# A two-layer graph network on one core: which engine copies the products out of PSUM, and how many tiles that engine fetches row by row

## The chip, the cores and the metric

The kernel runs on one core of a Trainium2 chip. The core has five engines with queues of their own: TensorE (PE), VectorE (DVE), ScalarE (ACT), GpSimd (POOL) and SyncE (SP, which here only issues transfers). Each engine works through its instructions in the order in which they were written. What is measured is the device time of one execution in microseconds (us), as the median of several runs. A comparison of this kernel can tell a difference of about 0.5% from none.

## The reference, cut to what matters

```python
# x: 50000 nodes x 128 floats; 850000 edges sorted by dst (400000 in both directions and 50000 self loops)
def layer(h, src, dst, rel, basis, w_comp, loop_w, bias):       # 16 relations, 8 bases
    W   = einsum('rb,bio->rio', w_comp, basis)
    agg = segment_sum(h[src], dst * 16 + rel)                   # sums of gathered rows by node and relation
    msg = einsum('nri,rio->no', agg.reshape(50000, 16, 128), W)
    return relu(msg + h @ loop_w + bias)
h = layer(x, ...1...); h = layer(h, ...2...)
out = layernorm(x + h)
```

What costs time is `h[src]`: in each layer one row of 512 bytes has to be fetched for each of the 800000 edges that are not self loops (self loops need no gather, since their row is the node's own).

## The kernel before, in words

The 800000 edges of a layer, sorted by destination, are cut into 6250 *tiles* of 128 edges. Five tiles are a *half chunk* (1250 a layer), two half chunks a *chunk* (625 a layer). `chunked()` runs over the two layers and, in each, over the chunks `c`. An order written out by hand (`tc.manual_schedule`) fixes the order on all five engines. The code that emits one tile also emits small steps of other work beside it (`beside`).

For each tile the 128 gathered rows come into a buffer `g` of 128 partitions. PE multiplies it with a matrix `hot` (L1145), which puts each edge's row into one of 12 local node columns for each of the 8 bases, weighted by the edge's relation. The five products of a half chunk fill one PSUM buffer `pa`; there are three such buffers. `taken_out()` (L1098 to L1101) copies a full `pa` to `aT` in SBUF. The call stands one tile late: it is emitted behind the first product of the next half chunk (L1154). In the first 8 and the last 8 chunks of a layer ScalarE makes this copy, in all others VectorE (`COPIED`, L1100).

Further work goes on beside: every fourth chunk PE multiplies `aT` with the bases (L816), ScalarE copies the result (`by_slot`, L821), PE transposes it (L826), VectorE spreads it (L799), and PE adds it into the nodes' sums (L861). For each group of 512 nodes the self loops are added (`hT` at L752, L766, L773, L781), and the group ends with a ReLU or a layer norm and a store (L883 to L896). VectorE makes the weights `hot` (L639, L668, L952).

Rows reach `g` on three ways. GpSimd fetches most tiles by one indirect gather of 128 rows each (L187). It fills a ring of 30 buffers (`RING * PER`); a slot is filled again when PE has used it, so the gathers run up to six half chunks ahead of PE. The row numbers for twenty tiles come from a ScalarE copy `at` (L1075). The last tile of some half chunks, though, is fetched row by row, as 128 transfers of 512 bytes, by SyncE or by ScalarE (`row_by_row`, L1048). Before every 32 rows the engine loads 32 addresses into registers (L1041) from the table `far` (L494). `takers()` deals these tiles out: SyncE takes the last tile of every ninth half chunk and so does ScalarE (`SPANS = (9, 9)`). That makes 136 tiles for SyncE and 135 for ScalarE in a layer. Their row transfers are spread evenly over the stretch of program that lies at least `LEAD = 8` half chunks ahead of the use. Each of the two engines has three buffers for such tiles. PE waits for the semaphore of a tile right at its product (L1145).

The tables of edges are made on the chip in groups (`rows_of`, L457). Group 0 holds the first 16 half chunks, group 1 the next 104. A generator `coming` makes the later groups a step at a time, and a loop at the head of a chunk (L1113) forces it to the end of a group when the group will soon be needed.

Of the kernel before, what the change touches and what calls it, by code (L numbers as in the profile page):

```python
# [60 lines left out]
LK = 64  # L61
LBITS = 10
FETCH = 2
WIDE = 20
AT = 8
PER = 5
Q = AT // 2
# [1 line left out]
WEIGHTS = AT * PER * 8  # L69
BITS_AT_ONCE = BANK - WEIGHTS  # L70
RING = 6
SPANS = (9, 9)
LEAD = 8
THEN = 3
COPIED = 8
HELD = 3
SEMS = 8
LOADED = 32
# [15 lines left out]
def tile_rgcn_resnorm(  # L94
# [15 lines left out]
    nc = tc.nc  # L110
# [4 lines left out]
    C = -(-M // (K * P))  # L115
# [4 lines left out]
    ROWS = list(range(0, 2 * C, P)) if 2 * C <= P else [0, FIRST, *range(P - 8, 2 * C, P)]  # L120
# [93 lines left out]
    uses = [0] * len(APART)  # L214
    earliest = (max(SPANS) + LEAD + 1) // 2 + 1
    far = consts.tile([P, len(ROWS), P], I32, name="far")

    def takers():

        of, first = {}, max(SPANS) + LEAD + 6  # L220
        for i, span in enumerate(SPANS):
            for q in range(first + span * i // len(SPANS), 2 * C - LEAD, span):
                while q in of:
# [388 lines left out]
    def chunked():  # L612
        with (
# [5 lines left out]
            def ks(c):  # L619
                return min(K, -(-M // P) - c * K)  # L620
# [26 lines left out]
            def told_apart(of, by, width, c, name):  # L647

                k = sum(ks(i) for i in range(c, min(c + Q, C)))
                apart = hp.tile([P, Q * K, width], U8, name=name, bufs=1)[:, :k]  # L650
                nc.vector.tensor_tensor(
                    apart,
                    of[:, None, :width].to_broadcast([P, k, width]),
                    by[:, c * K : c * K + k, None].to_broadcast([P, k, width]),
                    op=OP.is_equal,
                )
                return apart
# [241 lines left out]
            def done(steps):  # L899
                for _ in steps:  # L900
                    pass
# [19 lines left out]
            ready, read_by, numbered_all = [0], {}, []  # L921
# [18 lines left out]
            for n, of in enumerate((x, H1)):  # L940
# [78 lines left out]
                def alone(t):  # L1019

                    return t % PER == PER - 1 and t // PER in taken_by

                def row_by_row(i):
# [3 lines left out]
                    mine = sorted(q for q in taken_by if taken_by[q] == i)  # L1027
                    for q, before in zip(mine, [mine[0] - SPANS[i], *mine]):
                        while now[1] < before - LEAD:
# [25 lines left out]
                        held[q * PER + PER - 1] = to, sem, 16 * P * (use // SEMS + 1), group  # L1055
                        assert now[1] < q

                def place_in_ring(t):

                    turn, k = divmod(n * tiles + t, RING * PER)  # L1060
                    return k if turn % 2 == 0 else k // PER * PER + PER - 1 - k % PER
# [7 lines left out]
                def numbers(b):  # L1069

                    m = min(WIDE, tiles - b * WIDE)
                    if m <= 0:
                        return
                    at = hp.tile([P, WIDE], I32, name="at", bufs=3)[:, :m]
                    made = nc.scalar.copy(at, src[:, b * WIDE : b * WIDE + m])  # L1075
                    for group in read_by.pop(len(numbered_all) - 3, ()):
                        tc.declare_no_dep(made.ins, group=group, reason="their rows were used before")
                    read_by[len(numbered_all)] = read_now = []
                    numbered_all.append(at)
                    numbered[b] = at, read_now  # L1080

                def fetch(some):

                    for t in some:
                        if t < tiles:
                            if t % WIDE == WIDE // 2:
                                numbers(t // WIDE + 1)
                            if not alone(t):
                                at, read_now = numbered[t // WIDE]
                                k, group = place_in_ring(t), f"tile{n}_{t}"  # L1090
# [5 lines left out]
                to_take = []  # L1096

                def taken_out():  # L1098

                    by_vector = COPIED <= now[0] < C - COPIED  # L1100
                    (nc.vector.tensor_copy if by_vector else nc.scalar.copy)(*to_take)  # L1101

                numbered, held = {}, {}
                numbers(0)
                now, made = [0, 0], [0]
                owning = own_of_all()
                copying = [row_by_row(i) for i in range(len(APART))]
                for c in range(C):
                    now[0] = c
                    if n == 0 and c:  # L1110

                        next(coming, None)
                        while ready[0] + 1 < len(ROWS) and 2 * min(C, c + FETCH + earliest) > ROWS[ready[0] + 1]:  # L1113
                            next(coming)
                    if c == 0:
                        fetch(range(RING * PER))
                        nc.vector.tensor_copy(table, COMP[n].rearrange("p r b -> p b r"))
                        weighing = weights(0)
                        done(weighing)
                        hots[0] = hot_of(0)  # L1120
                        hots[1] = hot_of(1)
                        if n == 0:
                            for _ in range(LBITS + 3):
                                next(first_runs)
                    if c % 2 == 0 and c + 2 < C:
                        weighing = weights(c + 2)
                    hot = hots.pop(c)
                    if c % BATCH == 0:
                        aTs[c // BATCH] = hp.tile([P, NB, BATCH * S], F32, name="aT")
                    aT, place_of = aTs[c // BATCH], c % BATCH * S  # L1130
                    if c > ALONE:
                        done(summing)
                        summing = sum_up(c - 1)
                    elif c % BATCH == 0:
                        summing = slots_of_batch(c - BATCH, aTs[c // BATCH - 1], st, n) if c else iter(())
                    for k in range(0, K, PER):
                        m = min(PER, ks(c) - k)
                        if m > 0:
                            pa = ps_a.tile([P, BANK], F32, name="pa")
                        for i in range(PER):  # L1140
                            now[1] = 2 * c + k // PER
                            if i < m:
                                t = c * K + k + i
                                row, sem, count, group = held.pop(t)
                                product = nc.tensor.matmul(  # L1145
                                    pa[:, i * NB * WN : (i + 1) * NB * WN],
                                    row,
                                    hot[:, k + i].rearrange("e b w -> e (b w)"),
                                    start=True,
                                    stop=True,  # L1150
                                ).wait_op(sem, count, "sem-ge")
                                tc.declare_fence(product.ins, group=group)
                                tc.declare_no_dep(product.ins, group=group, reason="it waits for their semaphore itself")
                            if i == 0 and c + k:  # L1154
                                taken_out()
                            if i == m - 1:
                                at = c * K + k + RING * PER
                                fetch(range(at, at + PER))
                                if n == 0 and c == 0 and k == 0:
                                    done(first_runs)  # L1160
                                to_take[:] = [
                                    aT[:, :, place_of + k * WN : place_of + (k + m) * WN].rearrange(
                                        "d b (i w) -> d i b w", w=WN
                                    ),
                                    pa[:, : m * NB * WN].rearrange("d (i b w) -> d i b w", i=m, w=WN),
                                ]
                                if c * K + k + m == tiles:
                                    taken_out()
                            beside(k + i, c, owning, summing, weighing)
                    if c + 2 < C:  # L1170
                        hots[c + 2] = hot_of(c + 2)
                    for one in added_in(c + 1) if c + 1 < C else ():
                        masks[one] = masks_of(one)
                    if n == 0 and c == 3:
                        beginning.close()
                    if n == 0 and c == C - 1:
                        done(coming)
                        count_up(pr)
# [199 lines left out]
```

## Time and profile before

| | |
|---|---|
| median of 3 runs | 23771.16 us (23735.37 to 23829.01) |
| the profiled execution | 23546.47 us, its span 23544.3 us |
| PE busy | 11586.5 us (49%) |
| VectorE busy | 11688.0 us (50%) |
| GpSimd busy | 11364.1 us (48%) |
| ScalarE busy | 838.5 us (4%) |

No engine is counted as busy for more than half of the span. The page does not count instructions that issue transfers, though, and SyncE and ScalarE issue 17408 and 17280 row transfers in each layer. Whether they are full is read from the timeline, where such rows stand as SPq and ACTq with the number of transfers and the time from the first to the end of the last.

### The profile page before, as it was taken

Reading aid. Unit: us, or ns where it says so; the run is one execution under the profiler, and the core shown is the slowest. Engines: PE = TensorE matmul, PEld = TensorE weight load, DVE = VectorE, ACT = ScalarE, POOL = GpSimd, SP = SyncE. Lnnn points to the kernel's source line nnn. Section 1 sums busy time; section 2 is a strip of 40 time slices with the busy share of each in tenths; the row PEclk is TensorE's granted clock in tenths of the full one; section 3 lists DMA queues with packets and bytes.
Section 4 is the critical chain, followed back from the end, with each engine's and each line's share of the span. In section 5 each row is a group of like instructions: output and inputs, shape, how many; then the busy total and the mean of one; then the engine's idle time right before and its main releaser. Section 6 shows DMA issues by size and latency. Waiting matters only on the chain. (4 is left out here: it accounts for less than half of the span.)

```text
span 23544.3 us, 262043 instructions
## 1 busy us (share of the span) xinstructions
PE 11586.5 (49%) x43954; PEld 7419.2 (32%) x43954; DVE 11688.0 (50%) x14173; ACT 838.5 (4%) x1873; POOL 11364.1 (48%) x11991
## 2 busy tenths in 40 slices
PE   4544445444554544444554444444544444444445
PEld 3333333333333333233333333332332333333233
DVE  5555555555544444444544444444444444444445
ACT  0000000000000000000000000000000000000000
POOL 5544445444544444444454444444444444444444
PEclk7776677776677676676767776776766777766767
DMA  2111111111111111111111111111111111111111
GB/s 58 50 47 43 46 46 49 48 44 44 47 44 40 40 39 40 39 39 39 42 45 43 42 42 42 42 42 41 42 42 42 43 42 41 42 41 42 42 42 41
DMA packets 591750, 1014.42 MB, mean 43 GB/s; under 512 B 270531, under 2 KB 342979, under 8 KB 583794
## 3 DMA queue, kind: packets, MB, share of 16 engines
q0 software_dynamic: 384528, 791.33, 13.3%
q1 hardware_dynamic: 133308, 186.60, 2.5%
q10 hardware_dynamic: 72208, 19.62, 0.4%
q14 instruction: 1353, 11.08, 0.2%
q8 instruction: 353, 5.78, 0.1%
HBM read 924.87 MB, written 71.59 MB: 42 GB/s over the span
## 5 line engine op out<-in xcount | busy, mean ns | idle before, releaser
L187 POOL DMA_INDIRECT g<-H,at x5979 | 5658.7, 946 | 6136.5 <-PE pa L1145 3621.1
L187 POOL DMA_INDIRECT g<-in_x_dram,at x5979 | 5680.7, 950 | 5939.1 <-PE pa L1145 3438.7
L1145 PE MATMUL pa<-hot,g 128*128 128x96 f32 x25000 | 4289.6, 317 | 5679.3 <-DMA g<-H 2934.2
L1145 PEld LDWEIGHTS pa<-hot,g 128*128 128x128 f32 x25000 | 4239.8, 236 | 7638.2 <-DMA g<-H 3007.6
L773 DVE TENSOR_TENSOR by<-po,lw 128x512 f32<-128x512 f32 x1568 | 1074.7, 686 | 6412.4 <-PE po L766 4721.4
L861 PE MATMUL pn<-slots,own 120*128 120x512 f32 x4128 | 2738.5, 789 | 2075.2 <-issue 1117.4
L816 PE MATMUL po<-aT,basis 128*128 128x480 f32 x4960 | 2572.1, 681 | 1366.1 <-DVE aT L1101 752.6
L766 PE MATMUL po<-basis,hT 128*128 128x512 f32 x3136 | 2118.3, 764 | 1753.8 <-ACT hT L752 924.0
L1101 DVE COPY aT<-pa 128x480 f32<-128x480 f32 x2436 | 1567.6, 648 | 2672.5 <-PE pa L1145 2143.6
L816 PEld LDWEIGHTS po<-aT,basis 128*128 128x128 f32 x4960 | 1122.5, 233 | 2626.5 <-issue 2478.6
L781 DVE TENSOR_REDUCE ls<-by 128x128 f32<-128x1152 f32 (+1 forms) x784 | 1653.6, 2109 | 549.1 <-DMA out_dram<-ls 444.1
L668 DVE TENSOR_REDUCE fixed<-terms 128x80 f32<-128x1280 f32 x1250 | 1864.6, 1492 | 30.3
L639 DVE TENSOR_TENSOR terms<-kinds,fixed 128x1280 f32<-128x1280 uint8 x1250 | 1848.2, 1479 | 10.9
L861 PEld LDWEIGHTS pn<-slots,own 120*128 120x128 f32 x4128 | 884.8, 243 | 2749.4 <-issue 1753.9
L952 DVE TENSOR_TENSOR hot<-fixed,own 128x960 f32<-128x960 f32 x1250 | 1438.7, 1151 | 21.3 <-remote 3.0
L766 PEld LDWEIGHTS po<-basis,hT 128*128 128x128 f32 x3136 | 595.2, 236 | 1803.4 <-ACT hT L752 936.8
L799 DVE TENSOR_TENSOR slots<-po,which 120x1024 f32<-120x1024 f32 (+1 forms) x630 | 760.9, 1208 | 441.4 <-remote 304.8
L826 PE MATMUL po<-ident,by_slot 128*120 128x128 f32 x1240 | 311.5, 343 | 743.5 <-DVE by L773 423.0
L1075 ACT CAST at<-src 128x20 int32<-128x20 uint16 x626 | 129.5, 207 | 12082.0 <-issue 8490.2
L826 PEld LDWEIGHTS po<-ident,by_slot 128*120 128x120 f32 x1240 | 190.9, 188 | 764.1 <-issue 634.0
L840 DVE TENSOR_SCALAR own<-col,node 120x256 f32<-120x256 f32 (+1 forms) x1250 | 423.2, 339 | 8.6 <-PE pn L861 7.9
L746 PE MATMUL po<-ident,h_own 32*128 32x32 f32 x3136 | 328.2, 249 | 60.1 <-issue 54.1
(144 smaller groups left out, 3556.2 us busy)
## 6 DMA issues: line engine op xcount, KB each, us to landing
g<-in_x_dram SPq DMA_DIRECT2D x17408, 0.5 KB
g<-H SPq DMA_DIRECT2D x17408, 0.5 KB
g<-in_x_dram ACTq DMA_DIRECT2D x17280, 0.5 KB
g<-H ACTq DMA_DIRECT2D x17280, 0.5 KB
g<-in_x_dram,at POOLq DMA_INDIRECT x5979
g<-H,at POOLq DMA_INDIRECT x5979
H<-ls SPq DMA_DIRECT2D x97, 256.0 KB
xw<-in_x_dram SPq DMA_DIRECT2D x97, 256.0 KB
```

The lines of the kernel that those rows point to most:

```text
L187: return nc.gpsimd.indirect_dma_start(out=to, out_offset=None, in_=of, in_offset=bass.IndirectOffsetOnAxis(ap=idx, axis=0))
L639: nc.vector.tensor_tensor(terms, kinds[:, :, None, :].to_broadcast([P, k, NB, NR]), table[:, None, :, :].to_broadcast([P, k, NB, NR]), op= ...
L668: nc.vector.tensor_reduce(to[:, : ks(i)], terms, AX.X, OP.add)
L766: nc.tensor.matmul(hb[:m], hT[:, j, :m], BASIS[n][:, b : b + few, :].rearrange("p b d -> p (b d)"), start=True, stop=True,)
L773: nc.vector.tensor_tensor(by[:m, b : b + few, :], hb[:m].rearrange("p (b d) -> p b d", d=D), lw[:m, j, g % T, b : b + few, None].to_broadc ...
L781: nc.vector.tensor_reduce(ls[:m, j, :], by[:m].rearrange("p b d -> p d b"), AX.X, OP.add)
L799: nc.vector.tensor_tensor(to[:k], of[:k, :, None, :].to_broadcast([k, pair, J, D]), which[:k, c : c + pair, :, None].to_broadcast([k, pair ...
L816: nc.tensor.matmul(ps[:, : BATCH * S], BASIS[n][:, b, :], aT[:, b, :], start=b == 0, stop=b == NB - 1)
L861: nc.tensor.matmul(sums[g], own, of[:k].rearrange("s j d -> s (j d)"), start=c == first(g), stop=c == final(g),)
L952: nc.vector.tensor_tensor(hot[:, : ks(c)], pm[:, : ks(c), :, None].to_broadcast([P, ks(c), NB, WN]), own[:, : ks(c), None, :].to_broadcast ...
L1101: (nc.vector.tensor_copy if by_vector else nc.scalar.copy)(*to_take)
L1145: product = nc.tensor.matmul(pa[:, i * NB * WN : (i + 1) * NB * WN], row, hot[:, k + i].rearrange("e b w -> e (b w)"), start=True, stop=Tr ...
```

## The change

Three things are changed. ScalarE makes all copies of `pa` to `aT`, at the same place of the order as before. SyncE still takes every ninth half chunk's last tile, ScalarE now every tenth; with that the first such tile of a layer is one half chunk later. And while group 0 of the tables is the only one, the loop that forces the next group looks 6 chunks ahead (`FETCH + SOONEST`) in place of 12 (`FETCH + earliest`), so that group 1 is forced in chunk 3 and not in chunk 1. The new assertions say when the tables have to be there and issue nothing.

```diff
+SOONEST = 4
-SPANS = (9, 9)
+SPANS = (9, 10)
-COPIED = 8
...
+                assert ready[0] + 1 == len(ROWS) or 2 * min(c + Q, C) <= ROWS[ready[0] + 1]
...
+                def known(t):
+
+                    return ready[0] + 1 == len(ROWS) or t // PER < ROWS[ready[0] + 1]
...
+                    assert n or known(b * WIDE + m - 1)
...
                 def taken_out():
 
-                    by_vector = COPIED <= now[0] < C - COPIED
-                    (nc.vector.tensor_copy if by_vector else nc.scalar.copy)(*to_take)
+                    nc.scalar.copy(*to_take)
...
-                        while ready[0] + 1 < len(ROWS) and 2 * min(C, c + FETCH + earliest) > ROWS[ready[0] + 1]:
+                        soon = FETCH + (earliest if ready[0] else SOONEST)
+                        while ready[0] + 1 < len(ROWS) and 2 * min(C, c + soon) > ROWS[ready[0] + 1]:
                             next(coming)
```

Since lines are added, a line of the changed kernel from L650 on has a number that is higher by one to six than that of the same line before.

The first place where the order differs is ScalarE in the middle of the first layer, around its sixtieth `by_slot` copy. Before, ScalarE's queue there holds row transfers (`g<-in_x_dram 1x512`), address loads (`far`) and few copies:

```order
L349 CAST word<-r_i 128x672
L1048 DMA g_121<-in_x_dram 1x512 x3
L1041 TENSOR_LOAD far
L1048 DMA g_121<-in_x_dram 1x512 x8
L1075 CAST at<-src 128x20
L1048 DMA g_121<-in_x_dram 1x512 x17
L821 COPY by_slot<-po 128x480
L1048 DMA g_121<-in_x_dram 1x512 x7
L1041 TENSOR_LOAD far
```

With the change it reads so:

```order
L1106 COPY aT<-pa 128x5x8x12
L1049 DMA g_121<-in_x_dram 1x512 x13
L1106 COPY aT<-pa 128x5x8x12
L1049 DMA g_121<-in_x_dram 1x512 x10
L1081 CAST at<-src 128x20
L1049 DMA g_121<-in_x_dram 1x512 x2
L1106 COPY aT<-pa 128x5x8x12
L1042 TENSOR_LOAD far
L1049 DMA g_122<-in_x_dram 1x512 x13
L822 COPY by_slot<-po 128x480
L1106 COPY aT<-pa 128x5x8x12
L1049 DMA g_122<-in_x_dram 1x512 x13
```

A copy of `pa` now stands behind every 12 or 13 row transfers, and no row transfer behind it is issued before PE has filled that `pa`.

The second place is VectorE at the start of the first layer, where the tables of group 1 are made (`104x640` and `104x128`; `far` holds the addresses from which SyncE fetches its first tile). Before:

```order
L639 TENSOR_TENSOR terms<-kinds,fixed 128x1280
L668 TENSOR_REDUCE fixed<-terms 128x80
L952 TENSOR_TENSOR hot<-fixed,own 128x960
L471 TENSOR_TENSOR both<-full,parts 104x640
L473 TENSOR_TENSOR word<-full,parts 104x640
L488 TENSOR_SCALAR src<-pa 128x4x104
L488 TENSOR_SCALAR src<-pa 128x104
L494 TENSOR_SCALAR far<-both 104x128
```

With the change:

```order
L639 TENSOR_TENSOR terms<-both_kinds,fixed 128x768
L716 TENSOR_REDUCE lw<-terms 128x48
L652 TENSOR_TENSOR kinds<-fixed,rel 128x640
L639 TENSOR_TENSOR terms<-kinds,fixed 128x1280
L669 TENSOR_REDUCE fixed<-terms 128x80
L652 TENSOR_TENSOR own<-fixed,key 128x480
L953 TENSOR_TENSOR hot<-fixed,own 128x960
L471 TENSOR_TENSOR both<-full,parts 104x640
L473 TENSOR_TENSOR word<-full,parts 104x640
L488 TENSOR_SCALAR src<-pa 128x4x104
L488 TENSOR_SCALAR src<-pa 128x104
L494 TENSOR_SCALAR far<-both 104x128
```

The table `far` of group 1 now comes behind the weights of chunks 2 and 3 and the first self-loop weights `lw`, which before came behind it.

## The prediction, made before the result was known

> **What bounds the kernel now.** I read the chain of waits first, then who waited for whom, then the timelines of the two engines that issue rows. On the page the chain of work that ended last goes by engine and line (SPq is SyncE's queue, ACTq ScalarE's):
>
> ```profile
> SPq 12%; issue 7%; PE 1%; ACTq 0%; DVE 0%; DMA 0%; ACT 0%; another core or an unknown queue 0%; DVEq 0%
> ```
>
> Where the chain is put down to a queue it is SyncE's, hardly ever ScalarE's. The table of waits (us in total, times, longest) says what PE and GpSimd wait for:
>
> ```profile
> POOL g L187 <- PE pa L1145: 7059.8, 728, 48.6
> ...
> PE pa L1145 <- DMA g<-H: 2934.2, 121, 41.5
> ...
> PE pa L1145 <- DMA g<-in_x_dram: 2288.7, 94, 38.6
> ```
>
> PE waits 215 times for a row buffer, 24.3 us each (5222.9 us), and there are 272 tiles that SyncE fetches. GpSimd waits for PE, because its ring is full when PE stands. So neither of them sets the pace. Is SyncE full? The longest of its own waits for others, and its timeline in the first layer:
>
> ```profile
> SPq L295 <- DVE picked L422: 59.2, 1, 59.2
> SPq L889 <- ACT ls L886: 43.4, 1, 43.4
> SPq L896 <- DVE pn L883: 23.3, 1, 23.3
> ...
> 9000.41 31.15 SPq L1048 DMA_DIRECT2D g<-in_x_dram  x64
> 9031.57 0.69 SPq L889 DMA_DIRECT2D H<-ls  x1
> 9032.98 69.84 SPq L1048 DMA_DIRECT2D g<-in_x_dram  x91
> ```
>
> It waits for almost nothing and issues without a break: 155 rows in 101.0 us, 0.652 us a row, 83.4 us for a tile of 128. A half chunk takes 23544.3 / 2500 = 9.42 us, nine of them 84.8 us. SyncE is full, and its tile every nine half chunks sets the pace.
>
> Why is a row so dear? Three stretches of SyncE, and what GpSimd did in them (POOL is the fifth busy column, with its gathers in brackets), and one address load from the chain:
>
> ```profile
> 9106.04 18.05 SPq L1048 DMA_DIRECT2D g<-in_x_dram  x42
> ...
> 9106.00:9124.00 18.00, 13.16 (x34) 7.02 (x35) 4.14 (x4) 0.56 (x1) 0.00 (x0) 0.71 0.01 2
> ...
> 9125.38 0.95 POOL L187 DMA_INDIRECT g<-in_x_dram,at  x1 [32.98 <-PE pa L1145]
> ...
> 9124.82 6.48 SPq L1048 DMA_DIRECT2D g<-in_x_dram  x13
> ...
> 9045.73 12.00 SPq L1048 DMA_DIRECT2D g<-in_x_dram  x8
> ...
> 9046.48 10.56 ACTq L1048 DMA_DIRECT2D g<-in_x_dram  x6
> ...
> 9046.00:9058.00 12.00, 3.13 (x10) 1.96 (x9) 3.65 (x4) 0.00 (x0) 8.03 (x9) 0.59 0.21 54
> ...
> 18825.06 2.22 SPq L1041
> ```
>
> With no gather, 42 rows take 18.05 us, 0.43 us each with the address loads. In the first 6.5 us of a run of gathers SyncE still issues 13. Some way into a run it issues 8 in 12 us beside 9 gathers, about one row for each gather, and ScalarE 6. So SyncE's pace hangs on how long GpSimd's runs are, and these on how PE stands and goes.
>
> **The change part by part.** *SyncE's rows.* Every ninth half chunk as before, 136 tiles a layer: nothing removed from the engine that sets the pace.
>
> *ScalarE's rows and copies.* ScalarE's timeline beside the above, the busy time of all engines in it (ScalarE is the fourth column), and the copy on either engine (mean ns of one behind the comma):
>
> ```profile
> 9001.11 19.25 ACTq L1048 DMA_DIRECT2D g<-in_x_dram  x38
> ...
> 9020.53 7.91 ACTq L1048 DMA_DIRECT2D g<-in_x_dram  x17
> 9028.48 1.07 ACT L752 COPY hT<-po 128x512 f32<-128x512 f32 x1 [7.82 <-PE po L746]
> 9036.71 0.56 ACT L821 COPY by_slot<-po 128x480 f32<-128x480 f32 x1 [7.16 <-PE po L816]
> 9036.78 24.30 ACTq L1048 DMA_DIRECT2D g<-in_x_dram  x37
> ...
> 9061.26 0.89 ACTq L1048 DMA_DIRECT2D g<-in_x_dram  x3
> ...
> 9062.27 41.91 ACTq L1048 DMA_DIRECT2D g<-in_x_dram  x57
> ...
> 9000.00:9104.00 104.00, 38.47 (x150) 25.62 (x150) 36.66 (x39) 2.68 (x5) 43.87 (x47) 0.65 0.14 35
> ...
> L1101 DVE COPY aT<-pa 128x480 f32<-128x480 f32 x2436 | 1567.6, 648 | 2672.5 <-PE pa L1145 2143.6 <-remote 460.9 <-PE po L746 32.6
> ...
> L1101 ACT COPY aT<-pa 128x480 f32<-128x480 f32 x64 | 35.6, 559 | 384.2 <-PE pa L1145 224.0 <-issue 98.6 <-remote 56.1
> ```
>
> ScalarE issues 152 rows in 94.26 us, 0.620 us a row, 79.4 us a tile. The change leaves it 122 tiles a layer (29, 39, ... in half chunks) for 135: 26 x 79.4 = 2064 us less issuing. It gains 2436 copies x 0.559 = 1362 us. In all it has 700 us less to do. At the present pace ten half chunks last 94.2 us; ScalarE has to fill 79.4 for its tile, 5.6 for ten copies and 838.5 / 2500 x 10 = 3.4 for what it computes already, 88.4 in all. Both are hidden by SyncE's pace, as long as a copy is not late (the second rival).
>
> *VectorE* loses 2436 x 0.648 = 1579 us. It is 50% busy and nothing in the chain above, so I count 0.
>
> *GpSimd* takes the 26 tiles: 26 gathers, each 0.95 us and 0.30 to the next, 32.5 us, in time in which it now waits for PE. For SyncE a gather costs, at the start of a run, (6.48 - 13 x 0.33) / 5 = 0.44 us, and deep in a run (12.00 - 8 x 0.33) / 9 = 1.04 us; 0.33 is the row without gathers once two address loads of 2.2 us are taken out of the 18.05. That is 11 to 27 us; I take **+20**.
>
> *The start.* SyncE's first rows wait for `far`:
>
> ```profile
> 97.77 0.29 DVE L494 TENSOR_SCALAR far<-both 104x128 int32<-104x128 f32 x1
> ...
> 103.93 33.28 SPq L1048 DMA_DIRECT2D g<-in_x_dram  x57
> ...
> 105.63 1.48 DVE L639 TENSOR_TENSOR terms<-kinds,fixed 128x1280 f32<-128x1280 uint8 x1
> ...
> 121.29 1.16 DVE L952 TENSOR_TENSOR hot<-fixed,own 128x960 f32<-128x960 f32 x1
> ```
>
> The work from 105.63 to 122.4 us now goes ahead of `far`, so SyncE begins up to 16.8 us later. Nothing is gained by it on SyncE, and an engine without breaks carries the delay to the end: 0 to 17, I take **+16**.
>
> *How the copies pace PE.* This is the term that decides. Between two tiles of SyncE PE now runs nine half chunks in 84.8 - 24.3 = 60.5 us, 6.7 us each, since VectorE frees `pa` at once. ScalarE needs 8.84 us for each half chunk after the change (88.4 / 10). PE can be ahead of the copies by three `pa`, 20 us. Over nine half chunks ScalarE falls back by 9 x 2.1 = 19 us. So PE is held once or so near the end of its run, arrives at SyncE's tile a few us later, and stands there the less. The total of gathers stays, but GpSimd's run is broken once more. Each break lets the first five gathers of the new run cost SyncE 0.44 in place of 1.04 us: 3.0 us. Against that, after a run the rows come slowly for a moment. Here a run's last gather began at 9091.46 us:
>
> ```profile
> 9091.68 1.42 SPq L1048 DMA_DIRECT2D g<-in_x_dram  x2
> ```
>
> That is 2 rows in 2 us where 6 were possible, 4 x 0.33 = 1.3 us lost, which leaves 1.7 us for a break. One more break for each of 272 tiles: **-460** us. The bounds are no more breaks (0) and three for each tile (-1390); I take one, by the 19 against 20 us.
>
> *Fewer rows of ScalarE beside SyncE's.* 3328 rows go. Bounds: 0, or each of those that fell into GpSimd's busy time (48%) lets one row of SyncE through for which it pays 0.33 us less later, -527 us. Deep in the run each queue got about one row for each gather, so a row less in one gives the other little; I take **0**. In the Trainium skill, the page DMA: Bandwidth & Descriptors, section Queues, rings and completion order, says that a DMA engine goes round between the queues that have work and changes only at packet borders. By that rule, too, SyncE gets its turn whether ScalarE's queue holds much or little, and only the round gets shorter; the 8 and 6 rows beside 9 gathers agree, and the sum would stay; by a sharing in which ScalarE's turns all go to SyncE it would fall by 527.
>
> The sum is 20 + 16 - 460 = -424 us on the profiled 23546.5, 1.80%, which gives 23122. The three timed runs have their median 1.0% above that execution, so the same share is taken from the median: 23771 x 0.982 = **23343**, say 23345 us.
>
> **The rivals.** *The pace stays.* PE is not held (ScalarE is ahead at the start of each run) and GpSimd's runs stay as they are. For it: SyncE keeps all its rows, and 728 waits of GpSimd for PE show that the runs are broken often already. Against it: ScalarE's 8.84 us against PE's 6.7. Then +36 us remain: 23771 x 23582.5 / 23546.5 = 23807. A change that in effect does nothing but shift idle time reads the same.
>
> *ScalarE becomes the bound.* A copy stands in ScalarE's queue behind 12 or 13 rows, and behind it the next rows; PE stands when three `pa` are not copied. At the start of the second layer the kernel before does both at once:
>
> ```profile
> 11866.43 15.53 ACTq L1048 DMA_DIRECT2D g<-H  x12
> ...
> 11883.26 0.56 ACT L1101 COPY aT<-pa 128x480 f32<-128x480 f32 x1 [1.05 <-issue]
> ...
> PE pa L1145 <- ACT aT L1101: 9.8, 1, 9.8
> ```
>
> There PE did wait for a copy. For the whole: the stretch of ScalarE above has 103.1 us, 94.3 of them issuing and 2.7 computing, so about 6.2 of waiting, 5.7 in 94.2. With that, 88.4 + 5.7 = 94.1 of 94.2 us are full: any new wait decides. If a copy waits for PE by half its own length, 0.28 us, ten half chunks need 96.9 us: +2.9%, 24460 us; 0.1 us each makes +0.95%, 23997. Against it: ScalarE's 6.2 us are mostly waits for PE, and these shrink when it falls behind PE; and PE's 24 us at each of SyncE's tiles are room in which ScalarE catches up. The Trainium skill speaks for this rival: the page PSUM — Partial Sum Buffer, section Engine vs sequencer instructions, calls the queues of ScalarE, VectorE and GpSimd strict FIFO, so that no copy passes a row transfer in front of it. The 9.8 us above agree.
>
> *ScalarE's turns go to SyncE.* The bound of -527 in full, beside the breaks: -951 us, 22811. Against it stand the 8 rows of SyncE beside only 6 of ScalarE.
>
> **How the numbers follow.** The pace is eased by shorter runs of gathers (23345; its own range 23000 to 23650): 0.50. The pace stays (23807): 0.22. ScalarE becomes the bound (23900 to 24460): 0.22. ScalarE's turns go to SyncE (22811): 0.06. By the 0.5% that can be told, faster is below 23652, slower above 23890. Faster gets the first and the last but 0.01, 0.55; no change the second, 0.22, and 0.01 of the first; slower the third, 0.22. The range goes from 22750, which takes in nearly two and a half breaks a tile, to 24100, which leaves out the dearer half of the third case.
>
> **What would show each step.** In the changed kernel's profile I look for these. ScalarE's copy at about 0.56 us x2500 and VectorE's busy time lower by 1.58 ms. SyncE still without waits, its rows x64 to x100 without a break, but under 0.64 us a row: if it is 0.65 again, the breaks did not come. PE's waits for row buffers under 5200 us in total, and a new row in which PE waits for ScalarE's copy. GpSimd waiting for PE oftener than 728 times, each time shorter. SyncE's first rows near 120 us. The prediction is wrong if PE's wait for copies grows past the 24 us that it now loses at each of SyncE's tiles, or if ScalarE's timeline shows its copies waiting for PE while SyncE's tiles are early.

## The result, and the profile after

The changed kernel takes 23873.07 us (median of 15 runs, 23805.8 to 23932.19), the kernel before 23778.34 us (15 runs, 23732.18 to 23829.01). The ratio is 1.0043, interval 1.0033 to 1.0053: slower by 0.4%, and within the 0.5% that were taken as no change. A faster kernel was forecast, 23345 us. The profiled span is 23866.1 us.

The chain of the changed kernel, and who waited for whom (us in total, times, longest):

```profile
SPq 6%; issue 4%; PE 0%; ACTq 0%; DVE 0%; ACT 0%; another core or an unknown queue 0%; DMA 0%; DVEq 0%
```

```profile
POOL g L187 <- PE pa L1151: 7359.5, 737, 41.5
ACT aT L1106 <- PE pa L1151: 4609.9, 613, 26.6
PE pa L1151 <- DMA g<-H: 2808.7, 124, 38.2
PE pa L1151 <- DMA g<-in_x_dram: 2478.7, 108, 37.3
PE pa L1151 <- ACT aT L1106: 853.5, 143, 26.8
```

SyncE still leads the chain. PE's waits for row buffers come to 5287.4 us (5222.9 in the profile of before), and all 232 of them stand at SyncE's tiles, none at ScalarE's. PE's wait for ScalarE's copy is there, 143 times and 6.0 us each. Whether it shortens the other waits can't be read from these two profiles: the one of before is 0.8% shorter than the shortest of the 15 runs. Two profiles of one chip follow further down.

SyncE's timeline, at the start and in the first layer, and the busy time of all engines beside the second stretch (VectorE is the third column, ScalarE the fourth, GpSimd the fifth):

```profile
118.52 81.42 SPq L1049 DMA_DIRECT2D g<-in_x_dram  x98
...
9000.13 73.78 SPq L1049 DMA_DIRECT2D g<-in_x_dram  x111
9074.00 0.33 SPq L724 DMA_DIRECT2D h_own<-in_x_dram  x1
9074.42 35.46 SPq L1049 DMA_DIRECT2D g<-in_x_dram  x41
...
9000.00:9104.00 104.00, 48.04 (x207) 31.12 (x205) 40.46 (x39) 8.47 (x16) 49.32 (x53) 0.70 0.14 37
```

SyncE begins at 118.5 us (103.9 before) and is as full as it was: 152 rows in 109.7 us. Over a whole layer a tile of SyncE takes 86.6 us in the first and 86.8 in the second (first row to last by the number of tiles); in the profile of before it was 85.0 and 86.2, in a second one, used further down, 86.6 and 86.9.

ScalarE's timeline beside it, and its group of copies on the page:

```profile
9010.61 15.37 ACTq L1049 DMA_DIRECT2D g<-in_x_dram  x13
9026.02 0.56 ACT L1106 COPY aT<-pa 128x480 f32<-128x480 f32 x1 [15.36 <-PE pa L1151]
...
9032.36 15.62 ACTq L1049 DMA_DIRECT2D g<-in_x_dram  x13
9048.02 0.56 ACT L1106 COPY aT<-pa 128x480 f32<-128x480 f32 x1 [17.46 <-issue]
```

```profile
L1106 ACT COPY aT<-pa 128x480 f32<-128x480 f32 x2500 | 1398.5, 560 | 13217.2 <-issue 6478.5
```

A copy stands behind 13 rows, which take 15 us beside gathers. That no copy passes them is what the Trainium skill says on its page PSUM — Partial Sum Buffer, section Engine vs sequencer instructions (ScalarE's queue is a strict FIFO); the 15.62 us of rows ahead of the copy at 9048.02 agree. The copies themselves cost what was forecast, 0.56 us each.

### The profile page after: what moved, and what is told of

Its sections match the earlier page's. It is cut to its first block, busy times and chain, and to the rows that moved or that the text cites. A ratio compares the mean times of both kernels' runs of the same rounds, so it can differ in the third digit from the quotient of the medians.

```text
span 23866.1 us, 256060 instructions
## 1 busy us (share of the span) xinstructions
PE 11614.7 (49%) x43954; PEld 7437.2 (31%) x43954; DVE 10300.6 (43%) x11737; ACT 2150.3 (9%) x4309; POOL 11362.4 (48%) x12017
## 5 line engine op out<-in xcount | busy, mean ns | idle before, releaser
L1151 PE MATMUL pa<-hot,g 128*128 128x96 f32 x25000 | 4396.0, 322 | 6821.6 <-DMA g<-H 2808.7
L1151 PEld LDWEIGHTS pa<-hot,g 128*128 128x128 f32 x25000 | 4288.9, 239 | 8859.9 <-issue 3391.1
L817 PE MATMUL po<-aT,basis 128*128 128x480 f32 x4960 | 2492.3, 664 | 1219.0 <-ACT aT L1106 793.3
L1106 ACT COPY aT<-pa 128x480 f32<-128x480 f32 x2500 | 1398.5, 560 | 13217.2 <-issue 6478.5
L884 DVE TENSOR_TENSOR pn<-pn,ls 128x512 f32<-128x512 f32 x98 | 68.0, 694 | 939.5 <-PE pn L862 408.9
```

Of the source, the lines that this page charges most:

```text
L817: nc.tensor.matmul(ps[:, : BATCH * S], BASIS[n][:, b, :], aT[:, b, :], start=b == 0, stop=b == NB - 1)
L1106: nc.scalar.copy(*to_take)
L1151: product = nc.tensor.matmul(pa[:, i * NB * WN : (i + 1) * NB * WN], row, hot[:, k + i].rearrange("e b w -> e (b w)"), start=True, stop=Tr ...
```

## The experiments

The kernel before was run again with each of them on the same chip, and the ratios are against those runs. Two profiles of the same kernel differ by up to 1.4% (spans of the kernel before of 23544.3 and 23864.6 us), so effects under 1% are read from the ratios and not from two profiles.

### The three parts of the change, each alone

```diff
# the tables only                       # e1
+SOONEST = 4
-while ready[0] + 1 < len(ROWS) and 2 * min(C, c + FETCH + earliest) > ROWS[ready[0] + 1]:
+soon = FETCH + (earliest if ready[0] else SOONEST)
+while ready[0] + 1 < len(ROWS) and 2 * min(C, c + soon) > ROWS[ready[0] + 1]:
# ScalarE's spans only                  # e2
-SPANS = (9, 9)
+SPANS = (9, 10)
# the copies only                       # e3
-by_vector = COPIED <= now[0] < C - COPIED
-(nc.vector.tensor_copy if by_vector else nc.scalar.copy)(*to_take)
+nc.scalar.copy(*to_take)
```

> The kernel before with the later forcing of the second group of tables alone. SyncE sets the pace: it starts some 15 us later (118 us in place of 104) and carries that to the end, +15 us, ratio 1.0006, no difference that can be told. ScalarE's copies are to blame for the whole loss: ratio 1.000 all the same; the two part in the next two runs.

> The kernel before with ScalarE's tile in every ten half chunks alone; VectorE still copies. If SyncE sets the pace and each queue gets its own turn beside a gather: 26 more gathers, +11 to +27 us, ratio 1.000 to 1.001. If ScalarE's turns go to SyncE: up to -527 us, ratio 0.978. If ScalarE's row issue were the bound: 0.9 of its rows, ratio about 0.93.

> The kernel before with all copies out of PSUM on ScalarE, tiles still every nine half chunks on both. ScalarE then has 79.4 + 9 x 0.56 + 3.0 = 87.5 us of work in the 84.8 us of nine half chunks. If SyncE alone sets the pace: ratio 1.000 to 1.005. If ScalarE becomes a second bound without the easing to ten: 87.5 / 84.8 = 1.03 or more, and PE's wait for ScalarE's copies grows past the 853 us that the changed kernel shows.

The tables alone: 23532.45 us against 23523.48, ratio 1.0002 (0.9993 to 1.0011). SyncE's first row is at 119.1 us there, and the interval holds the 16 us that this was to cost. The spans alone: 23638.33 us, 1.0046 (1.0032 to 1.0060), +115 us where 11 to 27 were expected. Those 115 us stand in SyncE's rows: its tile takes 85.9 us on average in that profile and 85.4 in that of the tables alone, which for 272 tiles makes 120 us. The copies alone: 23594.92 us, 1.0028 (1.0017 to 1.0038). PE's waits for rows and for the copies in that kernel:

```profile
PE pa L1144 <- DMA g<-H: 2356.4, 117, 33.7
PE pa L1144 <- DMA g<-in_x_dram: 1902.0, 92, 35.4
PE pa L1144 <- ACT aT L1100: 926.4, 170, 26.7
```

So no part gains, and the copies, which were to bring the gain, cost 71 us. They do shorten PE's waits at SyncE's tiles, to 4258.4 us from 5222.9 in the profile of before (23544.3 us, this one 23597.8), but nothing comes of it. The three parts do not add up: alone they cost 0.02, 0.46 and 0.28%, together 0.43%.

### Does SyncE's tile set the pace?

```diff
-SPANS = (9, 9)
+SPANS = (10, 9)
```

> The kernel before with SyncE's tile in every ten half chunks and ScalarE's in every nine: the mirror of the eased ScalarE. If SyncE sets the pace (86 us a tile) a tile of ten half chunks takes the same 86 us plus 4.5 more gathers at 0.4 to 1.0 us: 88 to 90 us for ten half chunks, 22000 to 22500 us, ratio 0.93 to 0.95. If something else is as tight (GpSimd's runs, ScalarE's 82 us of work in nine half chunks): ratio 0.97 to 1.00.

21963.9 us, ratio 0.9328 (0.9314 to 0.9341). The waits in it:

```profile
POOL g L187 <- PE pa L1145: 5123.6, 686, 32.2
PE pa L1145 <- DMA g<-H: 1459.4, 77, 35.5
PE pa L1145 <- DMA g<-in_x_dram: 1249.0, 65, 34.4
```

SyncE took 88.7 to 89.0 us for a tile, a little more than before, but had ten half chunks for it: 8.8 us each in place of 9.4. PE's waits for row buffers halve, and all of them still stand at SyncE's tiles. That SyncE sets the pace is shown, and the gain lies in its share, the one number that the change left as it was.

### Do shorter runs of gathers ease SyncE?

Behind the five gathers of each half chunk GpSimd gets nine, or four, operations that compute nothing and only break the run.

```diff
+paced = hp.tile([P, 224], F32, name="paced", bufs=1)
...
+for _ in range(9):          # 4 in the second kernel
+    nc.gpsimd.iota(paced, pattern=[[1, 224]], base=0, channel_multiplier=0, ...)
```

> The kernel before with nine small iotas behind each half chunk's gathers. On the first kind of chip: ratio 0.91 if a break in a run of gathers is worth 1.7 us to SyncE; 1.00 if only the number of gathers counts. On the second kind GpSimd sets the pace: 1.486 as measured, and SyncE's rows stay at 0.33 us.

> The kernel before with four GpSimd operations that compute nothing behind the five gathers of each half chunk (nine of them made every run five gathers long, eased SyncE's rows beside gathers to 0.55 us, and cost GpSimd 3.3 us a half chunk, which then set the pace at 9.38 us). Four cost about 1.5 us. By the theory that a row's price hangs on the length of the run of gathers: GpSimd needs 5 x 1.25 + 1.5 = 7.7 us a half chunk, 19.3 ms, and is no longer the bound; SyncE's tile of nine half chunks needs 58 us without gathers and some 45 gathers beside it, about 0.55 x 128 = 70 to 75 us, 7.8 to 8.3 us a half chunk: 19500 to 20800 us, ratio 0.82 to 0.88. By the rival that the eased rows came of GpSimd's slowness as a whole (fewer gathers in a microsecond, not broken runs), SyncE's tile stays at 80 us or more: ratio 0.95 to 1.00. On a chip on which rows cost 0.33 us beside gathers, GpSimd sets the pace: 19300 us, 1.22 of the kernel before there.

With nine: 23460.09 us, ratio 0.9862 (0.9846 to 0.9878). With four: 19275.5 us, ratio 0.8195 (0.8175 to 0.8215). The chain and the group of the added operations with nine, and with four the chain, SyncE's timeline and the busy time beside it (GpSimd's column counts gathers and added operations):

```profile
POOL 37%; issue 10%; PE 2%; DMA 1%; ACTq 0%; DVE 0%; ACT 0%; POOLq 0%; DVEq 0%
...
L1161 POOL IOTA paced<- 128x224 f32 x22500 | 7223.4, 321 | 1392.3 <-POOL paced L1161 0.8
```

```profile
SPq 27%; issue 15%; POOL 3%; PE 2%; DVE 1%; DMA 1%; ACTq 0%; ACT 0%; another core or an unknown queue 0%; POOLq 0%; DVEq 0%
...
9002.93 58.89 SPq L1049 DMA_DIRECT2D g<-in_x_dram  x108
...
9000.00:9100.00 100.00, 58.61 (x228) 35.68 (x229) 55.98 (x61) 3.42 (x7) 74.81 (x114) 0.78 0.18 51
```

Nine operations fill GpSimd, which then sets the pace at 9.4 us a half chunk. With four a half chunk takes 7.7 us, and SyncE still leads the chain: its tile takes 69.9 us, nine half chunks 69.4, and PE still waits for it 181 times. But it issues 108 rows in 58.9 us, 0.55 us with the address loads, though GpSimd gathers faster than before (11958 gathers in 19282 us; the same number in 23865 before). Over the whole kernel, between two rows without a load, a row beside gathers and ScalarE's rows takes 0.92 us in the kernel before, 0.55 with nine operations and 0.56 with four. (A row is counted as beside gathers when a gather began in the 1.25 us before it.) So it is not GpSimd's slowness as a whole that eases SyncE.

These runs leave a rival: within a stretch of gathers the four operations also thin them out, to five in 7.6 us instead of five in 6.25. The kernel before answers it, where nothing is added. Its gathers start every 1.25 us; a *run* ends where the next starts over 2.6 us after the last. This is what one of SyncE's rows takes (us, beside ScalarE's rows, second profile of the kernel before), by the gather of the run that it stands beside:

| gather of its run | 1, 2 | 3, 4 | 5, 6 | 7 to 9 | 10 to 14 |
|---|---|---|---|---|---|
| all runs | 0.43 | 0.85 | 1.15 | 1.64 | 2.00 |
| runs whose first gather comes 1.4 to 2.3 us late | 0.45 | 0.87 | 1.16 | 1.61 | 1.98 |
| runs whose first gather comes over 8.7 us late | 0.41 | 0.88 | 1.21 | 1.74 | 1.98 |

The price climbs with each gather of a run, and a break of about 2 us brings it back as far as a long one. With four operations the break is 1.4 us, with nine 3.3.

### Did the change bring such breaks?

The kernel before and the changed one, profiled again on one chip.

> The changed kernel once more. On the first kind of chip: ratio 1.004 as before. On the second kind, where rows cost 0.33 us and before is held by ScalarE (its eased twin ran at 0.967): 26 tiles fewer on ScalarE, 60 us of work in ten half chunks, 11984 gathers of 1.25 us = 14980 us: 15100 to 15400 us, ratio 0.96 to 0.98. If ScalarE's copies hold PE there: ratio 1.00 or more.

23891.43 us, ratio 1.0045 (1.0032 to 1.0059). GpSimd's waits for PE and PE's waits for rows and copies, of the kernel before and then of the changed one:

```profile
POOL g L187 <- PE pa L1145: 7260.3, 722, 50.1
PE pa L1145 <- DMA g<-H: 3049.4, 120, 39.9
PE pa L1145 <- DMA g<-in_x_dram: 2499.7, 100, 40.5
```

```profile
POOL g L187 <- PE pa L1151: 7350.5, 758, 42.1
PE pa L1151 <- DMA g<-H: 2766.2, 123, 38.3
PE pa L1151 <- DMA g<-in_x_dram: 2437.6, 107, 36.9
PE pa L1151 <- ACT aT L1106: 705.0, 122, 26.6
```

36 waits more, where 272 were forecast. Counted from the starts of all gathers, there are 1223 runs before and 1246 after; two profiles of the kernel before differ as much from each other (1197 and 1223). SyncE's rows beside gathers and ScalarE's rows take 0.92 us before and 0.90 after. So the runs hardly changed, nor did the price. PE's waits at SyncE's tiles did get shorter, 5203.8 us after 5549.1, as PE was held by copies before it came there.

Why does PE's hold not stop GpSimd? The first profile of the changed kernel has the answer in large part. When one of the 143 holds begins, GpSimd still has 8.1 gathers on average whose ring slots PE has already freed, 10 us of work at 1.25 us each, and in 124 cases this lasts longer than the hold. In 80 of the 143 (56%) GpSimd does stop once these are issued. But it does so nearly as often where nothing holds PE: in 51% of the 2170 half chunks whose first product did not wait. No run changed the size of the ring.

### What ScalarE's rows cost SyncE

Thin ScalarE's tiles much more, or move them by one half chunk with no work added or taken:

```diff
-SPANS = (9, 9)
+SPANS = (9, 18)                                                        # g4
-for q in range(first + span * i // len(SPANS), 2 * C - LEAD, span):
+for q in range(first + (span * i + 1) // len(SPANS), 2 * C - LEAD, span): # h1
```

> The kernel before with the spans (9, 18): only ScalarE's tiles are thinned out, from every ninth to every eighteenth half chunk; some 135 tiles go to GpSimd, SyncE keeps its own. (9, 10) moved 26 tiles and cost 115 us, 4.4 us a tile, of which the price of a gather for SyncE, 0.44 to 1.04 us, explains 11 to 27. If 4.4 us is what a moved tile costs wherever it goes: +600 us, ratio 1.025. If only the price of the gathers counts, 135 x 0.44 to 1.04 = 60 to 140 us: 1.003 to 1.006. If thinner ScalarE rows ease SyncE, below 1. On a chip on which rows are cheap beside gathers 0.967, as measured there.

> The kernel before with the spans (9, 9) as they are, but ScalarE's tiles five half chunks behind SyncE's instead of four (SyncE's tiles then follow ScalarE's by four, where it was five). No work is added or removed. With the spans (9, 10) the distance runs through all values, and SyncE's mean time for a tile was, by distance from ScalarE's tile before it, 86.6 to 87.8 us at one to four half chunks and 85.1 at five (profiles of the changed kernel; 84.6 to 87.5 and 85.6 in that with the spans alone, each uncertain by about 1 us). By the theory that (9, 10) costs 0.46% because it gives up a good fixed distance, four makes each of SyncE's tiles 1.5 to 2.5 us longer: 272 x 2 = +540 us, ratio 1.015 to 1.03. By the rival that the distance plays no part and the cost comes of the 26 tiles moved, 0.998 to 1.002. On a chip on which rows are cheap beside gathers this says nothing.

(9, 18): 23336.81 us, ratio 0.9917 (0.9893 to 0.9941). Moved by one: 23830.93 us, 1.0010 (0.9999 to 1.0021).

The first of these edits does more than its expectation says. In `takers()` the first tile of both engines comes `max(SPANS) + LEAD + 6` half chunks into the layer, so with (9, 18) SyncE begins nine half chunks later and fetches 135 tiles in a layer, not 136. A tile takes 85.2 and 85.6 us in the two layers, much as before, so by an estimate the two tiles are 171 of the 183 us gained. The 12 us that are left lie within the interval: that thinner rows of ScalarE are worth more than the 138 added gathers cost is not shown.

Row by row there is an easing: SyncE's rows beside gathers take 0.73 us where ScalarE issues none and 0.90 where it does, and at the same place of a run, the fifth gather, 0.69 and 1.00. In the Trainium skill, the page DMA: Bandwidth & Descriptors, section Queues, rings and completion order, has the DMA engine go round between the queues that have work; a round that gets shorter without ScalarE's queue agrees with that, 0.90 to 0.73 us, and it is not the full turn of ScalarE that SyncE gains.

A distance of four half chunks between the two engines' tiles is as good as five; no other was tried alone. Why (9, 10) costs 0.46% stays open: a price for each moved tile does not explain it, since in (9, 18) 136 moved tiles cost nothing that can be told.

### The same kernels on another chip

Four kernels ran on a chip on which the kernel before takes 15758.97 us (15757.29 to 15767.42, 9 runs): the changed kernel with wider spans, the kernel before with (9, 18), and the kernel with nine operations.

> The changed kernel with a tile in every twelve half chunks on both SyncE and ScalarE. SyncE sets the pace: a tile costs it about 50 us without gathers and 0.8 to 0.9 us for each of 58 gathers, 98 us in twelve half chunks, 8.2 us each, 20400 us, ratio 0.86. If GpSimd cannot take the 134 more gathers at that pace, or PE is held by ScalarE's copies (79.4 + 12 x 0.92 = 90 us in twelve half chunks): ratio 0.90 or more.

> The changed kernel with a tile in every eighteen half chunks on both. By SyncE: 50 + 88 x 0.85 = 125 us in eighteen half chunks, 6.9 us each, about PE's own 6.7 us between its waits: 17300 us, ratio 0.73, if nothing else stands in the way. With GpSimd at 4.9 x 1.25 = 6.1 us a half chunk plus its other waits, and PE, VectorE and ScalarE waiting for each other, more likely 0.75 to 0.85; the waits then name the next bound.

> The kernel before, with nine small iotas into a scratch tile on GpSimd (about 2.7 us) behind each half chunk's five gathers: the same gathers, but no run of more than five or six. It computes nothing new. My term (a break in a run of gathers is worth 1.7 us to SyncE): some 1300 more runs, -2200 us, ratio 0.91, with GpSimd then 8.7 us busy in a half chunk. If breaks ease SyncE nothing and only the number of gathers counts: ratio 1.00, or more where GpSimd comes late.

> The kernel before with ScalarE's tile in every eighteen half chunks alone: 134 tiles fewer on ScalarE, 134 more gathers. If a tile moved from ScalarE to GpSimd costs SyncE only its gather (0.8 to 1.0 us): +110 to +135 us, ratio 1.005 to 1.006. If the 4.4 us a tile of the run with every ten hold (115 us for 26 tiles): +590 us, ratio 1.025. If ScalarE's turns go to SyncE: ratio 0.9 or less.

(12, 12) after the change: 15227.85 us, 0.9661 (0.9647 to 0.9676). (18, 18) after it: 15395.03, 0.9767 (0.9752 to 0.9782). (9, 18) before it: 15235.83, 0.9668 (0.9655 to 0.9681). Nine operations: 23417.56, 1.4858 (1.4835 to 1.4880). SyncE's timeline in the run with (9, 18), and the busy time beside it:

```profile
5010.04 25.15 SPq L1048 DMA_DIRECT2D g<-in_x_dram  x63
...
5000.00:5060.00 60.00, 48.71 (x180) 30.28 (x178) 43.20 (x46) 1.81 (x5) 45.36 (x49) 0.83 0.25 64
```

GpSimd gathers without a break, 49 in 60 us, and SyncE still issues a row in 0.40 us with the loads (0.33 without, over the kernel). A gather costs SyncE next to nothing there, and GpSimd's own gathers are the limit: 12096 of 1.25 us, 15.1 ms of the 15.2. The changed kernel itself did not run on that chip.

### Versions that beat both

Wider spans for the two engines, on chips of the first kind.

```diff
-SPANS = (9, 10)     # the changed kernel; (9, 9) in the kernel before
+SPANS = (12, 12)    # f3
+SPANS = (18, 18)    # g2; g3 is the kernel before with it; h2 is g2 with two added operations
```

> The changed kernel with twelve half chunks on both engines. On the first kind of chip SyncE sets the pace, 50 us and 58 gathers of 0.8 to 0.9 us in twelve half chunks, 20400 us, ratio 0.86. On the second kind GpSimd sets it with 12517 gathers of 1.22 us: ratio 0.966 as measured.

> The changed kernel with the spans (18, 18): SyncE and ScalarE each take a tile every eighteen half chunks, GpSimd gathers the rest (12230 gathers). On a chip on which rows are dear beside gathers: SyncE needs 45 + 0.83 to 0.92 us for each gather that runs beside its tile; in eighteen half chunks there are 88 gathers, 118 to 126 us, 6.6 to 7.0 us a half chunk, against GpSimd's own 12230 x 1.25 = 15.3 ms, 6.1 us a half chunk. So 16400 to 17500 us, ratio 0.69 to 0.74, with SyncE and GpSimd close together. By the rival that the ScalarE queue of rows, not SyncE's, comes to set the pace once copies stand in it, 19000 us or more. On the other kind of chip 15395 us, as measured there.

> The kernel before with the spans (18, 18): as the run above, but VectorE copies out of PSUM and the tiles' order and due times are those of before. It tells what the copies and the order are worth when the pace is fast. If copies on ScalarE cost as they do alone at the old pace (0.28%), this is within 0.5% of the run above, a little faster. If at 6.5 us a half chunk copies that stand behind rows in ScalarE's queue hold PE, it is 2% or more faster than the run above. If VectorE, which then has 11.9 ms of work instead of 10.3, is late with the one-hot rows, it is slower than the run above.

> The changed kernel with the spans (18, 18) and two GpSimd operations that compute nothing behind each half chunk's five gathers. From nine and four of them a half chunk took GpSimd 9.38 and 7.71 us: 0.334 us each, 6.37 without, 7.04 with two. If a break of 0.7 us clears what has piled up as one of 1.5 us did (rows at 0.55 us), SyncE's tile needs some 75 to 90 us of the 18 x 7.04 = 127, GpSimd sets the pace: 17600 to 17800 us, ratio 0.75, faster than 18160 without the break. If gathers pile up as long as more than about 0.65 of them start in a microsecond (it was 0.65 with four operations, and is 0.71 here), the rows stay near 1.0 us and the time is that without the break plus what GpSimd loses: 18200 to 18800.

| | us | ratio to the kernel before |
|---|---|---|
| after, (12, 12) | 20943.34 | 0.8806 (0.8791 to 0.8820) |
| after, (18, 18) | 18159.78 | 0.7720 (0.7701 to 0.7738) |
| before, (18, 18) | 18426.33 | 0.7829 (0.7810 to 0.7848) |
| after, (18, 18), two added operations | 18307.14 | 0.7695 (0.7683 to 0.7707) |

At (12, 12) SyncE still sets the pace: 101.2 us a tile, 8.4 us a half chunk. At (18, 18) it does not. Its tiles are there 63 us before their use on average, and the chain of the changed kernel with (18, 18) reads:

```profile
PE 18%; DVE 14%; another core or an unknown queue 11%; issue 8%; ACTq 2%; ACT 0%; POOL 0%; DVEq 0%; DMA 0%; POOLq 0%
```

16400 to 17500 us were expected, with SyncE and GpSimd at the limit; what holds it at 18160 goes by PE and VectorE and was not followed further. Here the copies are worth something: with them on ScalarE the kernel is 1.4% faster (18159.78 against 18426.33 on the same chip), where at SyncE's pace they cost 0.28%. (The two kernels differ in the tables too, which alone changed nothing at the old pace.) Two added operations, breaks of 0.6 us, leave SyncE's rows beside gathers at 0.88 us (1.03 without them) and change the time by no more than the two intervals leave open.

## Why the prediction was wrong

*What bounds the kernel* was right: SyncE's tile sets the pace (0.9328 when it gets ten half chunks).

*Why a row is dear* was right: the price hangs on the length of the runs of gathers (0.43 us a row at their start, 2.00 beside the tenth gather and later; 0.92 on average, 0.56 with each run broken after five). The 1.7 us for a break were not too much either. With four operations there are some 1270 runs more and 4244 us less, 3.3 us for each by this estimate.

*ScalarE's rows and copies, VectorE.* The copies take 0.56 us x2500, as forecast. VectorE's busy time fell from 11688.0 to 10300.6 us, by 1387 where 1579 were forecast. That VectorE gains nothing was right.

*The start.* +16 us, within the interval of the tables alone.

*GpSimd's 26 tiles.* Forecast at +20 us; the spans alone cost 115, in dearer rows of SyncE. This term was mis-sized, and its cause is open.

*Fewer rows of ScalarE beside SyncE's: 0.* Right for this change, for a reason not given: in the two profiles of one chip ScalarE issued some 19000 rows beside gathers before and 19500 after, and those it lost all came from stretches without gathers (15600 before, 11700 after). The 0.9917 of (9, 18) does not speak against it, since nearly all of that is SyncE's two tiles fewer.

*How the copies pace PE* is the step that failed: "PE is held once or so near the end of its run ... GpSimd's run is broken once more", -460 us. PE is held: 143 times for 272 tiles of SyncE, 6.0 us each, and mostly where it was forecast (92 times in the seventh to ninth half chunk behind such a tile). PE does stand there the less, 5203.8 us after 5549.1 on one chip. But GpSimd's runs are not broken more for that: 1223 before and 1246 after where 272 more were forecast, and the price of a row stayed. When a hold begins, GpSimd has 10 us of freed slots to fill, and it stops behind a hold hardly oftener than elsewhere. The forecast took one engine's wait for another's without asking whether the ring between them passes it on.

The sum that set one break a tile, 19 against 20 us, was off as well. The 24.3 us are the mean of the 215 tiles at which PE waits. Over all 272 it waits 19.2, runs a half chunk in 7.3 us and not 6.7, and ScalarE falls back by 14 us, not 19. That agrees with a hold at only every second tile.

The nearest case was *the pace stays*, 23807 us: GpSimd's runs stayed as it said, though PE was held, which it had ruled out. The 66 us above it are less than what the spans alone cost above their estimate. That the range of 22750 to 24100 holds the result is owed to this rival and not to the step that was forecast. *ScalarE becomes the bound* did not happen: SyncE leads the chain, and all of PE's waits for rows stand at its tiles. *ScalarE's turns go to SyncE* did not either.

## What to carry to other kernels

When one engine sets the pace, ask first what its own share of the work is worth: here one number, a tile every ten half chunks instead of nine, brought 6.7%, while moving work between the engines that wait brought nothing. A stall that is to break another engine's run has to be longer than what the buffers between the two hold; work that out before counting on it. Count what an edit really moves: a wider span for ScalarE also took two tiles from SyncE here, and these were nearly the whole gain. Time a change again when the bound has moved: the same copies cost 0.28% at SyncE's pace and gained 1.4% past it.

## What the runs showed of the hardware

The same program took 23.5 to 23.8 ms on three chips and 15.76 ms on a fourth, which was used in one series of runs only. On the fourth a row of 512 bytes issued beside gathers takes SyncE 0.33 us; on one of the three it takes 0.92, from 0.43 at the start of a run of gathers to 2.00 beside the tenth and later, and 0.34 to 0.36 without gathers. Why the fourth differs was not tried. So a share of rows that is tuned on one chip can be far off on another: operations that do nothing made the kernel 18% faster on one of the three, and nine of them 49% slower on the fourth. A break of 1.4 us behind each fifth gather brought the row from 0.92 to 0.56 us, one of 3.3 us to 0.55, and one of 0.6 us, at the spans (18, 18), from 1.03 to 0.88.
